# Layer 0's first product takes x unnormalized: the mean moved into the weights, the deviation's factor behind the product

## The chip, the core and the metric

The kernel runs on one core of one Trainium2 chip. The core has five engines with instruction queues of their own: TensorE (PE in the profile; its weight loads are PEld), VectorE (DVE), ScalarE (ACT), GpSimd (POOL) and SyncE (SP), which here only issues DMA transfers. The metric is the time of one execution on the device in microseconds.

## The reference, cut to what matters

Two layers of a graph network with a mixture of experts, on 3327 nodes with 256 features. The layer norm has no weights:

```python
def _layernorm(x, axis=-1, eps=1e-5):
    m = jnp.mean(x, axis=axis, keepdims=True)
    v = jnp.var(x, axis=axis, keepdims=True)
    return (x - m) / jnp.sqrt(v + eps)

def _L0_gnn_ref(x, adj, W, b):
    support = jnp.matmul(x, W)                 # 3327 x 256, the "node features" s
    out = jnp.matmul(adj, support) + b
    return jax.nn.relu(out)

x = x + _L0_gnn_ref(_layernorm(x), adj, W, b)
x = x + _L0_ffn_ref(_layernorm(x), ...)        # 8 experts, top 2, hidden 1024
x = x + _L1_gnn_ref(_layernorm(x), adj, ...)   # tanh filter, top 700, two weights
x = x + _L1_ffn_ref(_layernorm(x), ...)        # 8 experts, top 2, hidden 256
```

What the change touches is the product `matmul(_layernorm(x), W)` of layer 0. For one row, (x - m) r W = r (x W - m 1W), with r = 1/sqrt(v + eps). Since m is the mean of x's row, x W - m 1W = x (W - M), where each column of M holds the mean of that column of W.

## The kernel before

The nodes are padded to 26 tiles of 128 rows. `x` lies in SBUF whole, as 128 partitions x 26 tiles x 256 features in f32, and so does `s`, the node features. The kernel is written in a framework that takes instructions in program order, gives each engine its own queue with a scheduler's order, and puts semaphores between engines. So an engine takes its instructions strictly in its queue's order; an instruction that waits holds up what stands behind it.

The order of the work:

1. SP loads x in seven transfers (L129), four tiles each, the last two; GpSimd loads the weights `proj_sb` (L226, through L213). Then SP fills the ring of six pieces (`ring`, 1664 KB each) with the transposed adjacency (L322).
2. GpSimd makes constants (L132 to L193): an identity for transposes, ones, masks, and counts that VectorE turns into f32 (the casts `blocks` L167, `ids` L184, `spare` L189, `slot` L193). The casts and GpSimd's next step wait for each other, and GpSimd issues small loads (L213 to L223) in between.
3. Layer 0's node features, a loop over pairs of tiles (L952 to L955). For each pair: VectorE takes mean and variance (`bn_stats` L254, `bn_aggr` L255), and one over the deviation by a bit trick and three Newton rounds in twelve more small operations (L257 to L266, tiles `ln_ve`, `ln_half`, `ln_guess`, `ln_nw`); VectorE then writes the normalized tile `xn` (L276); TensorE transposes it in 128x128 blocks to PSUM (L288, `pt`); ScalarE copies it to SBUF (L289, `xnT`); TensorE multiplies by the weights (L296, `ps_s`, two products of 128x256 for a tile), and ScalarE copies the result into `s` (L299). There are two `pt` and two `xnT` buffers, and four PSUM buffers for products (tag `py`).
4. The aggregation over 13 panels of 256 nodes (`aggregate`, L326 to L349): 52 f32 products for a panel from the ring and `s` (L340, `ps_g`), while VectorE normalizes finished tiles and routes them to experts, GpSimd scatters the rows to DRAM, and ScalarE counts positive entries of the adjacency (L962).
5. The experts of layer 0 in blocks of 256 rows (L785, L797, L839), the layer between (`between`, L1090), layer 1's aggregation and its experts.

`node_features` (L292) is called by layer 0's loop and, with other weights, by layer 1 (`second_features`, L1073); `statistics` (L246) is called by all four layer norms. An f32 product of 128x256 stands in the profile as two records.

Of the kernel before, what the change touches and what calls it, by code (L numbers as in the profile page):

```python
# [10 lines left out]
F32 = mybir.dt.float32  # L11
BF16 = mybir.dt.bfloat16
I32 = mybir.dt.int32
AF = mybir.ActivationFunctionType
ALU = mybir.AluOpType
# [7 lines left out]
P = 128  # L23
NT = 26
NP = NT * P
D = 256
DC = D // P
# [6 lines left out]
RING = 6  # L34
# [41 lines left out]


BEGUN, FIRST_TILES = 6, 14
FREE_PAN = NPAN - RING // NCHUNK
assert K * EARLY_PAN * PW >= E * (SB - 1) + EARLY * SB  # L80
PAIRS = [(t, 2) for t in range(0, NT, 2)]
# [4 lines left out]
def gnn_moe_two_layers(  # L86
# [24 lines left out]
    nc = tc.nc  # L111

    const = ctx.enter_context(tc.tile_pool(name="const", bufs=1))
    state = ctx.enter_context(tc.tile_pool(name="state", bufs=1))
    work = ctx.enter_context(tc.tile_pool(name="work", bufs=3))
    dram = ctx.enter_context(tc.tile_pool(name="dram", bufs=1, space=bass.MemoryType.DRAM))
    psh = ctx.enter_context(tc.tile_pool(name="psh", bufs=2, space=PSUM))
    psy = ctx.enter_context(tc.tile_pool(name="psy", bufs=4, space=PSUM))
    pst = ctx.enter_context(tc.tile_pool(name="pst", bufs=2, space=PSUM))

    x = state.tile([P, NT, D], F32, name="x")
    s = state.tile([P, NT, D], F32, name="s")

    ring = [state.tile([P, PIECE], F32, name=f"ring{i}") for i in range(RING)]
    cum = state.tile([P, NT + 1, E], BF16, name="cum")

    for t in range(0, NT, 4):
        n = min(4, NT - t)
        nc.sync.dma_start(out=x[:, t : t + n, :], in_=x_in[:, t : t + n, :])  # L129


    ident = const.tile([P, P], F32, name="ident")  # L132
    make_identity(nc, ident)
    ones = const.tile([P, 1], F32, name="ones")
    nc.gpsimd.memset(ones, 1.0)
    ones_sq = const.tile([P, P], BF16, name="ones_sq")
    nc.gpsimd.memset(ones_sq, 1.0)

    before = const.tile([P, P], BF16, name="before")
    nc.gpsimd.memset(before, 1.0)  # L140
# [1 line left out]
        out=before,  # L142
        in_=before,
# [66 lines left out]
    def by_feature(name, w, t=None):  # L210
        if t is None:
            t = const.tile([P, DC, w.shape[1]], F32, name=name)
        nc.gpsimd.dma_start(out=t, in_=w.rearrange("(c p) n -> p c n", p=P))  # L213
        return t

    def on_all_partitions(name, b):
        t = const.tile([P, b.shape[1]], F32, name=name)
        nc.gpsimd.dma_start(out=t, in_=b.partition_broadcast(P))
        return t
# [3 lines left out]
        nc.gpsimd.dma_start(out=t, in_=a)  # L223
        return t

    proj_sb = by_feature("proj_sb", g0_w)  # L226
    gnn_b_sb = on_all_partitions("gnn_b_sb", g0_b[0:1, :])
    f0_bg_sb = on_all_partitions("f0_bg_sb", f0_bg[0:1, :])
    gate = state.tile([P, E, D], F32, name="gate")
# [16 lines left out]
    def statistics(t0, n, kept=None):  # L246


        st = work.tile([P, n, 6], F32, name="ln_st")
        mv, guess = kept or (  # L250
            work.tile([P, n, 2], F32, name="ln_mv"), work.tile([P, n], I32, name="ln_guess")
        )
        for g in range(n):
            nc.vector.bn_stats(out=st[:, g, :], in_=x[:, t0 + g, :])  # L254
            nc.vector.bn_aggr(out=mv[:, g, :], in_=st[:, g, :])  # L255
        ve = work.tile([P, n], F32, name="ln_ve")
        nc.vector.tensor_scalar(ve, mv[:, :, 1], EPS, None, ALU.add)  # L257
        half = work.tile([P, n], I32, name="ln_half")
        nc.vector.tensor_scalar(half, ve.bitcast(I32), 1, None, ALU.logical_shift_right)
        nc.vector.tensor_scalar(guess, half, -1.0, float(0x5F3759DF), ALU.mult, ALU.add)  # L260
        rs = guess.bitcast(F32)
        nw = work.tile([P, n], F32, name="ln_nw")
        for _ in range(3):
            nc.vector.scalar_tensor_tensor(nw, rs, -0.5, rs, ALU.mult, ALU.mult)
            nc.vector.tensor_tensor(nw, nw, ve, ALU.mult)
            nc.vector.scalar_tensor_tensor(rs, nw, 1.5, rs, ALU.add, ALU.mult)  # L266
        return mv, rs

    def layernorm(t0, n, stats=None, at=0, xn=None):


        mv, rs = stats or statistics(t0, n)
        if xn is None:
            xn = work.tile([P, n, K, RW], F32, name="xn")
        for g in range(n):
            last_normalized[:] = [nc.vector.tensor_scalar(  # L276
                xn[:, g, 0, 0:D], x[:, t0 + g, :], mv[:, at + g, 0:1], rs[:, at + g : at + g + 1],
                ALU.subtract, ALU.mult,
            )]
        return xn  # L280

    def by_features(xn, n):

        xnT = work.tile([P, DC, n * P], F32, name="xnT", bufs=2)
        pt = pst.tile([P, DC, n * P], F32, name="pt", tag="pt")
        for g in range(n):
            for c in range(DC):
                nc.tensor.transpose(pt[:, c, ts(g, P)], xn[:, g, 0, ts(c, P)], ident)  # L288
        nc.scalar.copy(xnT, pt)  # L289
        return xnT  # L290

    def node_features(i, lhsT, w_sb):  # L292

        ps = psy.tile([P, D], F32, name="ps_s", tag="py")
        for c in range(DC):
            nc.tensor.matmul(  # L296
                ps, lhsT=lhsT[:, c, :], rhs=w_sb[:, c, :], start=(c == 0), stop=(c == DC - 1)
            )
        return nc.scalar.copy(s[:, i, :], ps)  # L299

    def add_relu(x_tile, ps, b_sb):

# [273 lines left out]
    def plan_early():  # L576


        early_rows[:] = rows_written
        nb = parts_of(tokens(EARLY_PAN * PW // P), SB - 1, "pl_nb")  # L580
        nb2, base2 = in_tiers(nb, None)
        end, past = steps(nb2, EARLY)
        v = work.tile([P, 3, 2 * E], F32, name="pl_v", bufs=1)
        ids_and_leads(v, nb2, base2, SB)
        sums = sums_before(past, v, EARLY, 2)
        row = work.tile([P, EARLY], F32, name="pl_row", bufs=1)
        nc.vector.tensor_tensor(row, slots[:, 0:EARLY], sums[:, 1, :], ALU.subtract)
        nc.vector.tensor_copy(early_table[:, 0, :], sums[:, 0, :])
        nc.vector.scalar_tensor_tensor(
            early_table[:, 1, :], sums[:, 0, :], float(NP), row, ALU.mult, ALU.add  # L590
        )
        took2 = work.tile([P, 2 * E], F32, name="pl_took2", bufs=1)
        taken(took2, nb2, end, EARLY)
        nc.vector.tensor_tensor(done, took2[:, 0:E], took2[:, E:], ALU.add)
# [105 lines left out]
    def experts(xlist, ys, group, fixed, n_hidden, func, w1T, b1, w2T, b2, copy, kept=None):  # L700
# [23 lines left out]
        def col_of(t):  # L724
            return t if t < EARLY else order[t - EARLY]

        def groups_of(t):
            return SG if t < EARLY or order[t - EARLY] < LATE_PAIRS else 1
# [6 lines left out]
        def load_one(late):  # L735
            t = len(loaded)
            table = late[0] if t >= EARLY else early_table
            col, n = col_of(t), groups_of(t)
            base = FREE_PAN * NCHUNK + t * places

# [196 lines left out]
    def fill(xlist):  # L937

        with tc.issue_after(last_piece[0].ins):
            for e in range(E):  # L940
                zeros = blk.tile([P, H // P, SB], F32, name="wide").rearrange("p h b -> p (h b)")
                zeros = zeros[:, 0 : SG * RW].rearrange("p (g d) -> p g d", g=SG)
                nc.gpsimd.memset(zeros, 0.0)
                nc.gpsimd.tensor_scalar(
                    zeros[:, :, ID], slot, float(AWAY + SPARE + (LATE + e) * SB), None, ALU.add
                )
                nc.sync.dma_start(
                    out=xlist[e * NP : e * NP + SB, :].rearrange("(g p) d -> p g d", p=P),
                    in_=zeros,
                )  # L950

    for t, n in PAIRS:  # L952
        xnT = by_features(layernorm(t, n), n)
        for g in range(n):
            last_feature = node_features(t + g, xnT[:, :, ts(g, P)], proj_sb)  # L955

    def count(pan, chunks):
        with tc.issue_after(last_feature.ins):
# [13 lines left out]
    def after0(pan):  # L972
# [9 lines left out]
        if pan == 1:  # L982
            fill(xlist1)
        if FREE_PAN <= pan < NPAN - 1:
            layer0.load(None)
# [12 lines left out]
    with tc.issue_after(last_product[0].ins):  # L998
# [9 lines left out]
        pc, lhsT=ones, rhs=positive.rearrange("p n i k -> p (n i k)"), start=True, stop=True  # L1008
# [35 lines left out]
    def begin():  # L1044
        for b in begun:
            add_loaded(*b)
        return statistics(0, BEGUN, begun_stats)
# [25 lines left out]
    def second_features(t, xnT):  # L1073
        n = 2
        h2T = work.tile([P, DC, n * P], F32, name="h2T", bufs=2)
        for oc in range(DC):
            ps = psh.tile([P, n * P], F32, name="ps_p", tag="ph")
            for c in range(DC):
                nc.tensor.matmul(  # L1079
                    ps,  # L1080
                    lhsT=proj_sb[:, c, ts(oc, P)],
                    rhs=xnT[:, c, :],
                    start=(c == 0),
                    stop=(c == DC - 1),
                )
            nc.scalar.activation(h2T[:, oc, :], ps, AF.Tanh, bias=g1_bp_sb[:, oc : oc + 1])
        for g in range(n):
            node_features(t + g, h2T[:, :, ts(g, P)], g1_wg_sb)
# [42 lines left out]
    def after1(layer1, pan):  # L1131
# [8 lines left out]
        if pan == EARLY_PAN:  # L1140
            plan_early()
        if FREE_PAN <= pan < NPAN - 1:
            for _ in range(NCHUNK):
# [35 lines left out]
    with tc.If(first_usual > 0) as arms:  # L1179
# [19 lines left out]
        with tc.If(second_usual > 0) as inner:  # L1199
# [6 lines left out]
            while len(layer1.started) < layer1.always:  # L1206
# [6 lines left out]
                if 0 <= k - 3 < len(first_tiles):  # L1213
                    t, n = first_tiles[k - 3]
# [175 lines left out]
```

## Time and profile before

| | |
|---|---|
| runs | 1262.30, 1259.44, 1262.47 us; median 1262.3 |
| profiled execution | 1255.26 us, of which the span from first to last instruction is 1253.5 |
| TensorE busy | 1201.3 us, 96% of the span |
| mean granted TensorE clock | 0.989 |
| layer 0's aggregation starts | 46.57 us into the span |

The span is cut into groups, waits and a chain. The chain of work that ended last is followed back from the last instruction, at each step to what released it. "Busy" of TensorE counts a matmul's record from start to end; records overlap. The granted clock is the share of full speed that the throttle allowed TensorE.

### The profile page before, as it was taken

What the parts mean: (1) busy time and instruction counts of PE and PEld (TensorE: products, weight loads), DVE (VectorE), ACT (ScalarE), POOL (GpSimd) and SP (SyncE); (2) the same over time, 40 slices, a digit from 0 to 9 for tenths busy, and PEclk for the clock granted to TensorE, in tenths of its full rate; (3) what the DMA queues carried; (4) which work ended last, traced back from release to release, by engine and by line L of the source; (5) the groups of instructions that cost most, each with busy time, mean ns of one, the idle gap of its engine ahead of it and who ended that gap; (6) DMA issues with size and microseconds to landing.
All of it is one profiled execution on the core that took longest, in us unless ns stands there. A gap on an engine that the chain in (4) does not pass through costs nothing.

```text
span 1253.5 us, 18523 instructions
## 1 busy us (share of the span) xinstructions
PE 1201.3 (96%) x5816; PEld 1035.3 (83%) x5816; DVE 712.2 (57%) x2919; ACT 519.3 (41%) x963; POOL 289.7 (23%) x363
## 2 busy tenths in 40 slices
PE   6999999999999999999999998999999999999992
PEld 5888888888888888888888887788888888877771
DVE  8267767677663111111111148668999998784454
ACT  3797455541022222323232234995455552043330
POOL 2023122131231111111111110302323223264432
PEclk9999999999999999999999998999999999999996
DMA  9676554454267655757566557244445542477696
GB/s 365 170 248 215 181 181 165 160 198 139 63 228 238 207 178 177 257 173 247 186 224 210 181 203 266 94 164 166 168 171 198 179 147 82 130 243 220 204 272 213
DMA packets 119546, 241.60 MB, mean 193 GB/s; under 512 B 21568, under 2 KB 89936, under 8 KB 112400
## 3 DMA queue, kind: packets, MB, share of 16 engines
q1 hardware_dynamic: 106624, 206.91, 50.3%
q0 software_dynamic: 11184, 31.85, 6.9%
q10 hardware_dynamic: 1632, 1.57, 0.4%
q8 instruction: 48, 0.79, 0.3%
q14 instruction: 58, 0.48, 0.1%
HBM read 203.99 MB, written 36.33 MB: 192 GB/s over the span
## 4 chain that ended last, share of the span: by engine, by line
PE 90%; DMA 4%; DVE 2%; issue 2%; ACT 1%; POOL 0%; SPq 0%; DVEq 0%; ACTq 0%; POOLq 0%
PE ps_g L340 47%; PE ps_y L839 18%; PE ps_h L797 18%; PE ps_s L296 4%; DMA ys<-wide,index 2%; DMA ring<-ys 2%; PE ptb L785 2%; PE ps_p L1079 1%; PE pt L288 1%; DVE x L916 0%; ACT xnT L289 0%; DMA x<-in_x 0%; DVE wide L846 0%; DVE ln_st L254 0%; POOL ys L464 0%
## 5 line engine op out<-in xcount | busy, mean ns | idle before, releaser
L340 PE MATMUL ps_g<-s,ring 128*128 128x256 f32 x2704 | 588.3, 380 | 0.0
L340 PEld LDWEIGHTS ps_g<-s,ring 128*128 128x128 f32 x2704 | 512.0, 190 | 68.7
L797 PE MATMUL ps_h<-xT,ring 128*128 128x256 f32 (+1 forms) x1176 | 252.6, 368 | 1.9 <-DVE xT L788 1.1
L797 PEld LDWEIGHTS ps_h<-xT,ring 128*128 128x128 f32 x1176 | 206.4, 190 | 39.7 <-ACT wide L804 4.7
L804 ACT ACTIVATE wide<-ps_h,ring 128x256 f32<-128x256 f32 (+1 forms) x240 | 110.1, 459 | 286.3 <-PE ps_h L797 278.1
L360 DVE SCALAR_TENSOR_TENSOR rt_product<-xn,gate 128x256 f32<-128x256 f32 x400 | 197.7, 494 | 12.4
L839 PE MATMUL ps_y<-ring,wide 128*128 128x256 f32 x896 | 200.3, 379 | 0.0
L464 POOL DMA_INDIRECT xlist<-xn,rt_idx x104 | 106.6, 1025 | 377.2 <-DVE ln_ve L257 301.7
L839 PEld LDWEIGHTS ps_y<-ring,wide 128*128 128x128 f32 x896 | 167.1, 190 | 21.0
L962 ACT ACTIVATE sign<-ring,below 128x416 bf16<-128x416 f32 x208 | 133.5, 642 | 72.6 <-DMA ring<-in_adjT 66.5
L464 POOL DMA_INDIRECT ys<-narrow,index x56 | 54.5, 972 | 331.4 <-DVE narrow L847 239.3
L788 DVE COPY xT<-ptb 128x512 f32<-128x512 f32 (+1 forms) x29 | 19.2, 663 | 153.5 <-PE ptb L785 153.5
L1110 ACT ACTIVATE ring<-ring 128x3328 f32<-128x3328 f32 x22 | 65.5, 2982 | 90.2 <-PE ps_g L340 37.2
L846 DVE TENSOR_TENSOR narrow<-ps_y,ring 128x256 f32<-128x256 f32 x56 | 23.8, 424 | 134.2 <-PE ps_y L839 132.7
L304 DVE TENSOR_TENSOR gnn_t<-ps_g,gnn_b_sb 128x256 f32<-128x256 f32 x52 | 21.9, 422 | 109.0 <-PE ps_g L340 96.3
L464 POOL DMA_INDIRECT ys<-wide,index x58 | 55.9, 965 | 63.4 <-DVE wide L847 40.3
L1111 ACT ACTIVATE ring<-ring 128x3328 f32<-128x3328 f32 x22 | 65.5, 2982 | 0.6
L804 ACT ACTIVATE narrow<-ps_h,ring 128x256 f32<-128x256 f32 (+1 forms) x64 | 28.9, 453 | 73.2 <-PE ps_h L797 54.7
L839 PE MATMUL ps_y<-s,narrow 128*128 x200 | 49.9, 390 | 5.5 <-issue 3.2
L425 ACT ACTIVATE rt_d<-rt_d 128x2 f32<-128x2 f32 x26 | 5.3, 202 | 115.2 <-DVE rt_d L424 115.2
L916 DVE TENSOR_TENSOR x<-x,ring 128x512 f32<-128x512 f32 (+1 forms) x36 | 30.2, 839 | 32.4 <-DMA ring<-ys 32.0
L839 PEld LDWEIGHTS ps_y<-s,narrow 128*128 128x128 f32 x200 | 35.4, 189 | 14.6 <-issue 8.6
(195 smaller groups left out, 1021.0 us busy)
## 6 DMA issues: line engine op xcount, KB each, us to landing
ring<-in_adjT SPq DMA_DIRECT2D x52, 1664.0 KB, 7.0
ring<-in_f_w1T SPq DMA_DIRECT2D x30, 1024.0 KB, 5.9
ring<-in_f_w2T SPq DMA_DIRECT2D x30, 1024.0 KB, 8.1
ring<-xlist SPq DMA_DIRECT2D x52, 258.0 KB, 2.9
ring<-in_f_w SPq DMA_DIRECT2D x36, 256.0 KB, 3.5
ring<-ys SPq DMA_DIRECT2D x13, 512.0 KB, 5.0
ring<-ys SPq DMA_DIRECT2D x5, 1024.0 KB, 5.5
ring<-in_f_b SPq DMA_DIRECT2D x34, 128.0 KB, 7.2
```

Of the source, the lines that this page charges most:

```text
L296: nc.tensor.matmul(ps, lhsT=lhsT[:, c, :], rhs=w_sb[:, c, :], start=(c == 0), stop=(c == DC - 1))
L340: nc.tensor.matmul(ps[it], lhsT=chunks[k][:, c, ts(it, P)], rhs=s[:, j, :], start=(j == 0), stop=(j == NT - 1),)
L360: nc.vector.scalar_tensor_tensor(product, xn[:, g, 0, 0:D], 1.0, gate[:, e, :], ALU.mult, ALU.mult, accum_out=sc[:, g, e : e + 1],)
L464: d = nc.gpsimd.indirect_dma_start(out=a[:, :], out_offset=bass.IndirectOffsetOnAxis(ap=index, axis=0), in_=rows_, in_offset=None,)
L785: nc.tensor.transpose(pt[:, c, ts(g, P)], xb[:, g, ts(c, P)], ident)
L797: nc.tensor.matmul(ps, lhsT=w1[:, c, ts(hc, P)], rhs=xT[:, c, :], start=(c == 0), stop=(c == DC - 1),)
L804: nc.scalar.activation(hT[:, hc, :], ps, func, bias=bb1[:, hc : hc + 1])
L839: last_product[:] = [nc.tensor.matmul(ps, lhsT=hT[:, hc, ts(g, P)], rhs=w2[:, hc, :], start=(hc == 0), stop=(hc == hc_n - 1),)]
L916: nc.vector.tensor_tensor(x_t, x_t, yt[:, :, k * D : (k + 1) * D], ALU.add)
L962: nc.scalar.activation(sign, a[:, :, ts(i, GROUP)], AF.Sign, bias=below, accum_out=positive[:, pan, i, k : k + 1],)
L1110: nc.scalar.activation(a, a, AF.Square)
L1111: nc.scalar.activation(a, a, AF.Tanh)
```

## The change

There are five parts. The first two tiles of x are loaded by a transfer of their own, then the weights on the same queue, then the rest of x. TensorE multiplies a tile of ones with itself 32 times at the very start, into a PSUM tile that nobody reads. The column means of the weights are made on TensorE (a matrix whose entries are all 1/256, kept for that time in the last piece of the ring, times the weights), and VectorE subtracts them from the weights in place. Layer 0 then transposes x itself, multiplies, and the copy from PSUM to `s` on ScalarE is an activation that multiplies each row by its r. Statistics are taken for batches of 2, 4, 4, 8 and 8 tiles instead of 2. And two temporaries of `statistics` are smaller: `ln_st` holds one tile, `ln_half` shares the space of `ln_nw`. The activation in `node_features` is used by layer 1 too, with a factor of 1.

```diff
+WARM = 32
...
-    for t in range(0, NT, 4):
-        n = min(4, NT - t)
+    proj_sb = const.tile([P, DC, D], F32, name="proj_sb")
+    for t, n in [(0, 2)] + [(t, 4) for t in range(2, NT, 4)]:
         nc.sync.dma_start(out=x[:, t : t + n, :], in_=x_in[:, t : t + n, :])
+        if t == 0:
+            nc.sync.dma_start(out=proj_sb, in_=g0_w.rearrange("(c p) n -> p c n", p=P))
+    ones_sq = const.tile([P, P], BF16, name="ones_sq")
+    nc.gpsimd.memset(ones_sq, 1.0)
+    warm = psy.tile([P, P], F32, name="ps_warm", tag="py")
+    for _ in range(WARM):
+        nc.tensor.matmul(warm, lhsT=ones_sq, rhs=ones_sq, start=True, stop=True)
     ident = const.tile([P, P], F32, name="ident")
     make_identity(nc, ident)
+    mean = ring[RING - 1][:, 0:P]
+    nc.gpsimd.memset(mean, 1.0 / D)
     ones = const.tile([P, 1], F32, name="ones")
     nc.gpsimd.memset(ones, 1.0)
-    ones_sq = const.tile([P, P], BF16, name="ones_sq")
-    nc.gpsimd.memset(ones_sq, 1.0)
...
-    proj_sb = by_feature("proj_sb", g0_w)
...
     def statistics(t0, n, kept=None):
-        st = work.tile([P, n, 6], F32, name="ln_st")
...
         for g in range(n):
-            nc.vector.bn_stats(out=st[:, g, :], in_=x[:, t0 + g, :])
-            nc.vector.bn_aggr(out=mv[:, g, :], in_=st[:, g, :])
+            st = work.tile([P, 6], F32, name="ln_st")
+            nc.vector.bn_stats(out=st, in_=x[:, t0 + g, :])
+            nc.vector.bn_aggr(out=mv[:, g, :], in_=st)
...
-        half = work.tile([P, n], I32, name="ln_half")
+        nw = work.tile([P, n], F32, name="ln_nw")
+        half = nw.bitcast(I32)
...
-        nw = work.tile([P, n], F32, name="ln_nw")
...
     def by_features(xn, n):
+        return turned_tiles([xn[:, g, 0, :] for g in range(n)])
+
+    def turned_tiles(tiles):
+        n = len(tiles)
         xnT = work.tile([P, DC, n * P], F32, name="xnT", bufs=2)
         pt = pst.tile([P, DC, n * P], F32, name="pt", tag="pt")
         for g in range(n):
             for c in range(DC):
-                nc.tensor.transpose(pt[:, c, ts(g, P)], xn[:, g, 0, ts(c, P)], ident)
+                nc.tensor.transpose(pt[:, c, ts(g, P)], tiles[g][:, ts(c, P)], ident)
         nc.scalar.copy(xnT, pt)
         return xnT

-    def node_features(i, lhsT, w_sb):
+    def node_features(i, lhsT, w_sb, scale=1.0):
...
-        return nc.scalar.copy(s[:, i, :], ps)
+        return nc.scalar.activation(s[:, i, :], ps, AF.Copy, scale=scale)
...
-    for t, n in PAIRS:
-        xnT = by_features(layernorm(t, n), n)
-        for g in range(n):
-            last_feature = node_features(t + g, xnT[:, :, ts(g, P)], proj_sb)
+    deviation = {}
+    for t0, n0 in [(0, 2), (2, 4), (6, 4), (10, 8), (18, 8)]:
+        _, rs = statistics(t0, n0)
+        deviation.update((t0 + g, rs[:, g : g + 1]) for g in range(n0))
+        for t in range(t0, t0 + n0, 2):
+            xT = turned_tiles([x[:, t + g, :] for g in range(2)])
+            if t == 0:
+                ps = psy.tile([P, D], F32, name="ps_mean", tag="py")
+                for c in range(DC):
+                    nc.tensor.matmul(
+                        ps, lhsT=mean, rhs=proj_sb[:, c, :], start=(c == 0), stop=(c == DC - 1)
+                    )
+                nc.vector.tensor_tensor(
+                    proj_sb, proj_sb, ps.unsqueeze(1).to_broadcast([P, DC, D]), ALU.subtract
+                )
+            for g in range(2):
+                last_feature = node_features(
+                    t + g, xT[:, :, ts(g, P)], proj_sb, deviation[t + g]
+                )
```

## The prediction

> **What bounds the kernel now.** I read the page first. TensorE is busy 96% of the span, and the chain that ended last is 90% TensorE. So a change that touches only the first 46 us can bring no more than what it takes from TensorE's idle or slow time there.
>
> ```profile
> span 1253.5 us, 18523 instructions
> PE 1201.3 (96%) x5816; PEld 1035.3 (83%) x5816; DVE 712.2 (57%) x2919; ACT 519.3 (41%) x963; POOL 289.7 (23%) x363
> PE 90%; DMA 4%; DVE 2%; issue 2%; ACT 1%; POOL 0%; SPq 0%; DVEq 0%; ACTq 0%; POOLq 0%
> ```
>
> Second, the chain in order of time over the first 110 us (start, length, what):
>
> ```profile
> 0.81 3.97 DMA x<-in_x
> ...
> 9.30 0.65 DVE xn L276 x2
> ...
> 11.42 0.42 DVE xn L276
> ...
> 11.89 1.11 PE pt L288 x4
> 13.00 5.97 PE ps_s L296 x16
> 18.96 0.45 PE pt L288 x4
> ...
> 19.50 0.59 ACT xnT L289
> 20.09 0.04 issue
> 20.14 3.72 PE ps_s L296 x16
> ...
> 46.57 44.89 PE ps_g L340 x208
> ```
>
> Three things are to be seen. x lands at 4.78, but the first product starts at 13.0, after VectorE's statistics and a detour to GpSimd. The products of tiles 0 to 3 (eight products, two records each) take 5.97 us where the next four tiles take 3.72: TensorE is at half pace until about 17.9. From 20.14 on each round of four tiles costs 4.89 us, and from 46.57 the aggregation runs without a gap. So the prize is how much earlier than 20.14 the products of tiles 4 to 7 start; everything behind shifts by that.
>
> Third, what idleness does to TensorE later: the windows from 756.4, where it waits for statistics between the layers (granted clock third from the end).
>
> ```profile
> 756.40:757.40 1.00, 0.01 (x1) 0.00 (x0) 1.00 (x6) 0.37 (x1) 0.00 (x0) 1.00 1.01 426
> 757.40:758.60 1.20, 0.00 (x0) 0.00 (x0) 1.06 (x7) 0.00 (x0) 0.00 (x0) 1.00 1.12 477
> 758.60:759.60 1.00, 0.00 (x0) 0.00 (x0) 0.83 (x6) 0.00 (x0) 0.00 (x0) 0.52 0.78 311
> 762.60:765.40 2.80, 2.80 (x9) 2.22 (x8) 2.73 (x8) 1.06 (x2) 0.00 (x0) 0.50 1.05 447
> ```
>
> Work ended at 756.4; by 758.6, 2.2 us later, the clock was halved; work resumed at 760.9 and the full clock came back at 765.4, 4.5 us after.
>
> **The change, part by part.** *Loads.* Two tiles of x go first, then the weights, on SP's queue. Before, 512 KB landed at 4.78, 0.9 us after that many bytes had moved (windows of the first 5 us: 66, 106, 246, 352, 385 GB/s in half-microseconds from 1.5). 256 KB had moved at 3.15, so two tiles land at about 4.1 and the weights at 4.8; the next tiles follow at 413 GB/s (6.1, 7.3, 8.6), ahead of need. The sixth ring load now waits for the mean products; only two small gate loads stand right behind it, ring data is not read before 40 us, and the transfers were saturated to 38 us anyway: nothing. On SP one more issue pushes the later loads back by its own 0.4 to 0.7 us, ahead of need; GpSimd loses an issue of 0.92 at 2.73, which nothing waits behind, and gains one 0.2 us memset: nothing.
>
> *Warming products.* 32 bf16 128x128 products from 1.05 (ones_sq is now GpSimd's first memset; memsets ended by 1.2 before). The trace has no such product. Lower bound 0.05 us each (bf16 products of 8 columns start 0.025 apart at full clock), upper 0.27 (first four f32 transposes, 1.09 us). I take 0.12: f32 transposes stand 0.45/4 = 0.11 apart at full clock, bf16 half of that, half clock twice. 32 x 0.12 = 3.8, so TensorE is free at 4.9; by the bounds at 2.7 or 9.7.
>
> *Mean products.* Two f32 products (four records at 0.43 slow, plus 0.2 drain): 1.9 us, 4.9 to 6.8. VectorE's queue reaches the subtraction at 4.1 + 0.80 (two bn_stats at 0.33 and an aggregate) + 7 dependent small operations at 0.20 = 6.3. So the subtraction starts at s = 6.8 and takes 0.65 (PSUM copies of that size 0.66). Transposes run 6.8 to 7.9, the copy on ScalarE ends near then, and the products of tiles 0 to 3 run from 8.0, at full clock (TensorE has been occupied since 1.05), to 11.7; transposes of 4 to 7 until 12.7. Until there the gain is 18.96 - 11.7 = 7.3 us.
>
> *The deviation behind the product: a new wait.* ScalarE's copies of s now carry the factor, and in the built order its queue reads: s of tiles 0, 1, then 2, 3, which wait for VectorE, and only then xnT of tiles 4 to 7. Statistics of tiles 2 to 5 are one batch, and its last operation is number 61 in VectorE's queue. Behind s: subtraction 0.65, six bn_stats at 0.33, fourteen small ones at 0.07 give 3.5 to the cast "blocks". Then the casts ids, spare and slot each wait for GpSimd, which in between issues DMAs:
>
> ```profile
> 10.13 0.26 POOL L172 TENSOR_SCALAR starts<-blocks 128x8 f32<-128x8 f32 x1 [6.48 <-DVE ln_nw L265]
> 10.89 0.25 POOL L182 IOTA wide_i<- 128x52 int32 x1
> 11.96 0.58 POOL L218 DMA_DIRECT2D f_bg_sb<-in_f_bg  x1
> 12.53 0.73 POOL L213 DMA_DIRECT2D f_r_sb<-in_f_rT  x1
> 13.26 0.16 POOL L191 IOTA wide_i<- 128x2 int32 x1
> ```
>
> Before, blocks to slot took 9.95 to 13.45 = 3.5 us; the new order (f_bg and f_r now ahead of the second iota) keeps the sum. The batch's rest is 1.2. Together s + 8.3. Then two s copies at 0.36 and one xnT copy of 0.59, with gaps 1.4: tiles 4 to 7 start at s + 9.7 = 16.5, against 20.14: 3.6 us earlier. Later batches (10.5 and 14.2 behind s) come before their tiles.
>
> *The clock.* TensorE then waits from 12.7 to 16.5, 3.8 us. By the row above, the clock is halved 2.2 us into such a gap and returns 4.5 us after work resumes. Of a 4.89 us round 3.72 are products, so the loss is 4.5 x 1/2 x 0.76 = 1.7. Bounds: 0 and 2.25 (5.97 - 3.72). I take 1.8, since tiles 4 to 7 meet the clock as the first four did.
> [...]
>
> *xn's scaling gone, ScalarE's copies.* 26 normalizations (0.33 each) leave VectorE; it was no longer the limit after 20 us, so nothing. COPY 128x256 takes 375 ns, ACTIVATE of that shape 473: 0.10 more for each s copy. In layer 0 ScalarE idles 0.49 before each, hidden. In layer 1 the same helper runs 26 times: 0 to 2.6 us; ScalarE is full only in 789 to 805 (9.82 of 10 us in 790 to 800), six copies there, half on the chain: 0.3.
>
> *Statistics' temporaries* (ln_half shares ln_nw, ln_st per tile) add no wait on another engine: nothing. The built order of the rest is unchanged but for one xlist load on SP.
>
> **Sum.** 3.6 - 1.8 - 0.3 = 1.5 us. The profiled execution took 1255.26 (1253.5 span and 1.8 around it); the runs' median is 1262.3, 0.6% above, so I take the difference off the median: 1260.8.
>
> **Rivals.** *Clock kept*: the gap is too short, or the first four tiles run slow themselves and fill it. For: warming products may not count as work, then tiles 0 to 3 end near 14 and the gap shrinks to about 1.5 us, while the start at 16.5 stays. Against: the 756 row. Gain 3.6 - 0.3 = 3.3, up to 4.3 if the mean products run fast too and x lands a little earlier: 1258 to 1259.
>
> *No wait for the statistics*: VectorE's batch comes in time, tiles 4 to 7 start 1.18 behind the first four (as 18.96 to 20.14 now), at 12.9: 7.2 - 0.3 = 6.9 us, 1255.4. For: the casts need not stall if GpSimd's issues are quicker. Against: without any stall the batch still ends at s + 7.3, so most of the wait stays.
>
> *Warming holds TensorE* (slower): at 0.27 each TensorE is free at 9.7, s is 11.6, tiles 4 to 7 start at 21.3, 1.2 later than now, with the slow clock 1.8 and 0.3: 3.3 slower, 1265.6, and 1267.9 with all layer-1 copies on the chain. It decides from 0.17 a product, where the gain is gone. For: TensorE starts slow. Against: bf16, and 0.025 between small ones.
>
> That the change does nothing is out: the built order has no xn in layer 0, and the first product's waits are changed as it says.
>
> **How the numbers follow.** The sum's case 0.40, clock kept 0.26, no wait 0.21, warming holds 0.13. What a measurement of this kernel can tell from no change is about 0.3%, 3.8 us: "no wait" and the upper half of "clock kept" (0.13) lie beyond it, and I count the slower case as beyond it too. Faster 0.34, same 0.53, slower 0.13. The range runs from 1255.2 to 1265.0; outside lie half of "no wait" and half of the slower case.
>
> **What would show it.** In the profile after: the first ps_s at about 8, not 13; 16 records in 3.7 us; then a TensorE wait of 3 to 4 us ended by ScalarE's xnT, itself behind s copies that wait for VectorE's ln_guess; clock 0.5 around 16 to 21; ps_g starting at 44 to 45. Wrong if ps_g starts below 41 (no wait), or above 46 (warming holds), or if a gap opens after 46 that is not there now.

## The result, and the profile after

The changed kernel takes 1262.39 us (median of 12 runs, 1260.0 to 1263.7), the kernel before in the same comparison 1262.38 (12 runs, 1259.44 to 1263.58). The ratio is 0.9997 with a 95% interval of 0.9989 to 1.0005: no difference that can be measured. The prediction said 1260.8, held no measurable change for the likeliest outcome, and its range held the time. But its sum of 1.5 us gained lies just outside the interval (which allows 1.4 gained at most), and the trace says more exactly that the sum failed: the aggregation starts half a microsecond later than before, not 1.8 earlier.

The page first: the same bound as before.

```profile
span 1260.6 us, 18469 instructions
PE 1207.1 (96%) x5852; PEld 1040.0 (82%) x5852; DVE 699.9 (56%) x2798; ACT 521.9 (41%) x963; POOL 289.5 (23%) x363
PE 90%; DMA 3%; issue 2%; DVE 2%; ACT 1%; POOL 1%; SPq 0%; POOLq 0%; ACTq 0%; DVEq 0%
```

The chain in order of time over the first 48 us of the changed kernel (start, length, what):

```profile
1.73 5.69 DMA x<-in_x
7.45 0.43 DVE ln_st L262
...
14.00 1.55 DVE slot L202
...
16.42 0.13 DVE ln_guess L274 x2
16.56 0.07 ACT s L311
...
16.93 0.47 ACT s L311
17.40 0.49 ACT xnT L301
17.93 6.45 PE ps_s L308 x16
...
25.54 3.73 PE ps_s L308 x16
...
47.08 1.08 PE ps_g L352 x5
```

This is the chain that the prediction described: statistics of tiles 2 to 5 in VectorE's queue, then the copies of `s`, then `xnT`, then TensorE. Tiles 4 to 7 start at 17.93 (20.14 before), but at half pace: 6.45 us for a round that takes 3.73 from 25.54 on. TensorE's timeline of the same stretch (start, duration, operation, in brackets the idle time before and its releaser) shows both the early success and the gap:

```profile
7.96 3.62 PE L308 MATMUL ps_s<-proj_sb,xnT 128*128 128x256 f32 x16
11.42 1.04 PE L300 MATMUL pt<-ident,x 128*128 128x128 f32 x8
17.93 6.44 PE L308 MATMUL ps_s<-proj_sb,xnT 128*128 128x256 f32 x16 [5.47 <-ACT xnT L301]
```

Tiles 0 to 3 run at 7.96 in 3.62 us (12.79 and 6.17 before, by the same view), so 7.5 us are won by 12.46, where the last transposes end. The gap of 5.47 us and the slow round behind it take all of it back.

The profiled spans differ by 7 us (1260.6 against 1253.5), but hardly from the change: layer 1's aggregation starts at 805.73 against 805.39. The stretch from there to the end is 454.9 against 448.1. It goes with the set of runs and not with the kernel: in the changed kernel's set both kernels take 1262 us, and in the later runs the stretch is 447 to 450 in eight profiles of two sets, 457 to 459 in the three of the third, whose runs of the kernel before also took 1265 us where those of the other sets took 1255. So experiments are judged here by the start of the two aggregations in their traces, and by ratios to runs of the kernel before on the same chip.

### The profile page after: what moved, and what is told of

The parts are those of the page before. It is cut to its first block, busy times and chain, and to the rows that moved or that the text cites. A ratio compares the mean times of both kernels' runs of the same rounds, so it can differ in the third digit from the quotient of the medians.

```text
span 1260.6 us, 18469 instructions
## 1 busy us (share of the span) xinstructions
PE 1207.1 (96%) x5852; PEld 1040.0 (82%) x5852; DVE 699.9 (56%) x2798; ACT 521.9 (41%) x963; POOL 289.5 (23%) x363
## 3 DMA queue, kind: packets, MB, share of 16 engines
q10 hardware_dynamic: 1632, 1.57, 0.4%
## 4 chain that ended last, share of the span: by engine, by line
PE 90%; DMA 3%; issue 2%; DVE 2%; ACT 1%; POOL 1%; SPq 0%; POOLq 0%; ACTq 0%; DVEq 0%
PE ps_g L352 46%; PE ps_y L851 18%; PE ps_h L809 18%; PE ps_s L308 3%; DMA ring<-ys 2%; PE ptb L797 2%; PE ps_p L1109 1%; DMA ys<-wide,index 1%; POOL ys L476 1%; DMA x<-in_x 0%; PE pt L300 0%; ACT xnT L301 0%; DVE x L928 0%; ACT s L311 0%; DVE ln_st L262 0%
## 5 line engine op out<-in xcount | busy, mean ns | idle before, releaser
L437 ACT ACTIVATE rt_d<-rt_d 128x2 f32<-128x2 f32 x26 | 5.3, 202 | 119.7 <-DVE rt_d L436 119.7
```

## The experiments

The table collects what the runs below showed: start and length of the products of tiles 4 to 7, the first `ps_g` of layer 0, the `ps_g` that opens layer 1's unbroken aggregation (all from TensorE's timeline, us), and, where timed, the ratio to the kernel before.

| kernel | tiles 4-7 | layer 0's `ps_g` | layer 1's | ratio (95%) |
|---|---|---|---|---|
| before | 20.14, 3.72 | 46.41 | 805.23 | |
| changed | 17.93, 6.44 | 46.91 | 805.56 | 0.9997 (0.9989 to 1.0005) |
| no factor | 13.80, 3.72 | 40.07 | 804.68 | 0.9987 (0.9975 to 1.0) |
| no warming | 18.90, 5.50 | 46.95 | 805.28 | |
| products in the gap | 18.43, 3.72 | 44.70 | 802.94 | 0.9992 (0.9983 to 1.0001) |
| casts moved + small batches | 14.70, 3.72 | 42.03 | 802.00 | 0.9984 (0.9964 to 1.0003) |
| casts moved | 17.68, 6.60 | 46.83 | 806.81 | |
| small batches | 16.77, 5.41 | 44.72 | 804.43 | |
| clearing doubled | 19.42, 6.14 | 48.12 | 806.54 | |
| no factor + SP's loads moved | 13.28, 3.72 | 39.55 | 798.21 | 0.995 (0.9935 to 0.9964) |
| SP's loads moved | 18.66, 5.88 | 47.09 | 806.93 | |
| both edits, finer, SP's loads moved | 14.51, 3.72 | 41.84 | 800.26 | 0.9961 (0.9948 to 0.9975) |
| the same, statistics paced | 13.12, 3.72 | 39.86 | 799.42 | 0.9945 (0.993 to 0.996) |

**Without the factor.** Is the gap the new wait for the deviation's factor, and what is the early start worth without it?

```diff
-                    t + g, xT[:, :, ts(g, P)], proj_sb, deviation[t + g]
+                    t + g, xT[:, :, ts(g, P)], proj_sb
```

> The deviation's factor is left out of the copies of s in layer 0 (the statistics are still computed, nothing waits for them), so layer 0's features are not scaled. In the changed kernel TensorE stood still from 12.46 to 17.93 and then ran tiles 4 to 7 in 6.45 us. Theory (the new wait for the factor takes the gain): no gap over 1 us, tiles 4 to 7 start at 12.9 and take 3.7, ps_g starts at 39.5 to 40 instead of 47.08, and the time falls by about 7 us, to 1255 to 1256. Rival (the early start meets another bound, x's later tiles or the ring's data): a new gap of 3 us or more opens between 13 and 46, ps_g starts at 43 or later. Rival (the gain is given back behind the first stage): ps_g at 40, but the time is within 2 us of the kernel before.

The gap is gone, and the first aggregation starts 6.8 us earlier than in the changed kernel. That part of the theory held. The time fell by only 0.13% (1.6 us, interval 0 to 3.1), not by 7: the second rival is right in what it says of the time, with a cause that no theory had named. It shows in TensorE's timeline ahead of the fifth panel, whose products start at 134.88:

```profile
107.70 22.69 PE L352 MATMUL ps_g<-s,ring 128*128 128x256 f32 x104
134.66 0.18 PE L458 MATMUL pr<-rt_both,before 128*128 128x8 bf16 x1 [4.27 <-DVE rt_both L409]
...
134.88 24.38 PE L352 MATMUL ps_g<-s,ring 128*128 128x256 f32 x104
```

The wait costs 4.27 us, and the panel behind it 1.69 more (24.38 for 22.69). Of the 6.8 us that leaves 0.9, which is what is left at layer 1 (804.68 against 805.56).

SP's queue (start, duration, transfers) shows where the wait comes from:

```profile
15.97 25.35 SPq L1008 DMA_DIRECT2D gate<-in_f_rT  x1
41.43 26.56 SPq L959 DMA_DIRECT2D xlist<-wide  x5
68.09 0.69 SPq L334 DMA_DIRECT2D ring<-in_adjT  x1
...
93.66 9.53 SPq L959 DMA_DIRECT2D xlist<-wide  x4
103.29 4.87 SPq L334 DMA_DIRECT2D ring<-in_adjT  x3
```

The issue of a gate load of 8 KB stands in the queue from 15.97 to 41.32, and 16 zero lists (GpSimd clears a buffer, SP writes it to DRAM), interleaved with ring loads, follow. In the lists of waits SP stands 35.3 us for GpSimd's `wide` (L956, up to 110 us), and GpSimd 42.3 us for earlier lists to land (L955, 12 times from 60 to 165), since there are two `wide` buffers. So a ring load is issued at 103.29 and lands at 111.67. ScalarE counts that piece from 111.75 on, and the small operation `rt_d` (L437, at 117.76) stands behind it in its queue. VectorE's routing waits for `rt_d` (18.1 us), and TensorE for VectorE.

**Without the warming products.** What do the 32 constant products buy?

```diff
-WARM = 32
+WARM = 0
...
-    warm = psy.tile([P, P], F32, name="ps_warm", tag="py")
     for _ in range(WARM):
-        nc.tensor.matmul(warm, lhsT=ones_sq, rhs=ones_sq, start=True, stop=True)
+        pass
```

> The 32 constant products at the start are left out; nothing else differs from the changed kernel. Theory (tiles 4 to 7 are held by the statistics, not by TensorE): the mean products start when x and the weights have landed, at about 4.5, so the subtraction stays within 0.3 of 6.56; tiles 0 to 3 take about 6 us instead of 3.62 and end at 14; tiles 4 to 7 start at 17.9 all the same, ps_g at 46.5 to 47.3. Rival (the warming is what brings the early start): everything from the first product on comes 2.3 or more later, ps_g at 49 or later.

The start of the aggregation is as expected (46.95 against 46.91), but by two misses that cancel. TensorE's timeline:

```profile
4.65 2.04 PE L975 MATMUL ps_mean<-proj_sb,ring 128*128 128x256 f32 x4 [4.65 <-DMA proj_sb<-in_g_w]
6.48 1.06 PE L299 MATMUL pt<-ident,x 128*128 128x128 f32 x4
7.87 1.11 PE L299 MATMUL pt<-ident,x 128*128 128x128 f32 x4 [0.33 <-DMA x<-in_x]
8.78 3.67 PE L307 MATMUL ps_s<-proj_sb,xnT 128*128 128x256 f32 x16
```

Tiles 0 to 3 are at full pace at 8.78 without any warming; I expected about 6 us for them. TensorE did nothing before 4.65; the mean products went at half pace (2.04 us), and 4.1 us after its first work it is at full pace, with nothing but the mean products and the transposes of x ahead. In three other runs, with the 32 products, the mean products took 1.10 us instead of 2.04, but then TensorE waited 2 us and more for x. The cost of the 32 is as small as their use, since without them TensorE waits for the weights till 4.65 anyway. Tiles 4 to 7 start at 18.90, 1.0 later than expected (VectorE waited 1.38 us for the fourth load of x, tiles 10 to 13), and lose less of the clock (5.50 against 6.44).

**Products in the gap.** Does the gap cost the clock?

```diff
+            if t == 2:
+                again = psh.tile([P, D], F32, name="ps_fill", tag="ph")
+                for _ in range(AGAIN):            # 4
+                    for c in range(DC):
+                        nc.tensor.matmul(
+                            again, lhsT=xT[:, c, P:], rhs=proj_sb[:, c, :],
+                            start=(c == 0), stop=(c == DC - 1),
+                        )
```

> Behind the products of tile 3 these products are done four times more, into a tile of PSUM that nobody reads: 16 records, 3.7 us at full clock, inside the gap of 5.47 us. Theory (the gap costs 2.7 us of clock on top of itself): the idle stretches left are 1.6 us or shorter, the granted clock stays at 1.0, tiles 4 to 7 start at 17.9 as before and take 3.7 instead of 6.45, ps_g starts at 44.3, the time falls by 2.7 us. Rival (the clock's fall does not come from the gap): tiles 4 to 7 take 6.4 again, ps_g stays at 47.

```profile
15.45 1.04 PE L301 MATMUL pt<-ident,x 128*128 128x128 f32 x8
18.43 3.72 PE L309 MATMUL ps_s<-proj_sb,xnT 128*128 128x256 f32 x16 [1.95 <-ACT xnT L302]
```

The round takes 3.72 instead of 6.44, though it starts 0.5 later (x landed later in this execution), and the aggregation starts at 44.70 (44.3 expected). In the trace the gain is still there at layer 1 (802.94, 2.6 less than in the changed kernel). The timed gain, 0.08% (1.0 us of the 2.7 expected), is too small for its interval to exclude zero. Work that nobody needs thus brings 2.2 us (44.70 against 46.91), only by keeping TensorE busy.

**Casts moved and small batches, together and apart.** What in VectorE's queue makes the factor late?

```diff
-    nc.vector.tensor_copy(blocks, count_i)        # and ids, spare, slot
+    nc.gpsimd.tensor_copy(blocks, count_i)
...
-    for t0, n0 in [(0, 2), (2, 4), (6, 4), (10, 8), (18, 8)]:
+    for t0, n0 in [(0, 2), (2, 2), (4, 2), (6, 4), (10, 8), (18, 8)]:
```

> The statistics of tiles 2 and 3 and of tiles 4 and 5 are two batches instead of one, and the four casts blocks, ids, spare and slot run on GpSimd instead of VectorE, so that no wait for GpSimd stands in VectorE's queue ahead of the factors. Theory (the queue ahead of the factors is what holds TensorE): the factor of tiles 2 and 3 is there at 12 to 12.7 instead of 16.5, tiles 4 to 7 start at 13 to 14 at full clock; a second, shorter gap of up to 2 us may open ahead of tiles 8 to 11, whose copies stand behind the factors of tiles 6 to 9; ps_g at 39.7 to 42, the time 5 to 7 us less than before. Rival (VectorE is slow in 13 to 16 whatever its queue holds, or GpSimd with the casts becomes late): tiles 4 to 7 start at 16 or later, ps_g at 45 or later.

Both together: tiles 4 to 7 start at 14.70 at full pace, the next round after a second gap of 1.35 (up to 2 was expected), `ps_g` at 42.03. The first and the last lie 0.7 and 0.03 beyond the theory's upper ends, far from the rival's 16 and 45. Of the 4.9 us won there, 3.6 are left in layer 1 (802.00), since the wait ahead of the fifth panel appears here too (1.36 us at 133.71). The timed gain, 0.16% (2.0 us), misses the 5 to 7 us expected, and its interval does not exclude zero.

The casts alone:

> Only the four casts blocks, ids, spare and slot go from VectorE to GpSimd; the statistics' batches are those of the changed kernel (factor of tiles 2 and 3 at 16.54 there). Theory (the casts and their waits hold the batch): VectorE saves two waits of 1.07 together, four casts of 0.5 or, with the slowed one, 2.1: the factor is there at 13.4 to 15, tiles 4 to 7 start at 14.8 to 16.4, ps_g at 42 to 46. Rival (the smaller batches did it all in the run with both edits): tiles 4 to 7 start at 17 or later.

Tiles 4 to 7 start at 17.68, the rival's number. Without the casts VectorE meets another hold at once, 1.52 us for the fourth load of x (tiles 10 to 13), whose statistics stand in its queue ahead of the last operations of the batch of tiles 2 to 5. That load landed at 13.66 in this execution; in the changed kernel's profile its statistics began at 11.90 without a wait. Without the 1.52 us the start would be 16.2 (an estimate by subtraction), inside the theory's range: this single execution does not decide between the two. This run also had the wait ahead of the fifth panel (1.12 us at 138.28), though its aggregation started no earlier: its ring load that stood at 99.04 in the changed kernel was issued at 106.88.

The batches alone:

> Only the batches of the statistics are smaller (2, 2, 2, 4, 8, 8 tiles); the casts stay on VectorE. Theory (two holds in one queue: the casts with GpSimd, and the batch with its late x; each alone suffices, as the run with the casts moved alone showed, where tiles 4 to 7 started at 17.68): the factor of tiles 2 and 3 still stands behind the cast slot and the slowed operations, is there at 15.6 to 16.2, tiles 4 to 7 start at 16.9 to 17.7, ps_g at 45.5 to 47. Rival (the batch alone is the hold): tiles 4 to 7 start at 14.7 as in the run with both, ps_g at 42 to 43.

Tiles 4 to 7 start at 16.77 and `ps_g` at 44.72, 0.1 and 0.8 below the theory's lower ends; the start is far from the rival's 14.7. So neither edit alone did it in these executions, and together they brought more than the sum of both (tiles 4 to 7 are 3.2 earlier; apart 0.3 and 1.2). That fits holds that stand one behind the other in one queue. The sizes are rough: each is one execution, and the fourth load of x landed at least 1.8 us later in one than in another.

**Clearing doubled.** In the changed kernel three operations behind the cast `slot`, and the cast itself, end only at 15.55. VectorE's timeline:

```profile
13.92 1.63 DVE L202 CAST slot<-wide_i 128x2 f32<-128x2 int32 x1
13.97 1.57 DVE L274 SCALAR_TENSOR_TENSOR ln_guess<-ln_nw,ln_guess 128x4 f32<-128x4 f32 x1
14.05 1.51 DVE L269 TENSOR_SCALAR ln_guess<-ln_nw 128x4 int32<-128x4 int32 x1
14.12 1.44 DVE L263 BATCH_NORM_AGGREGATE ln_mv<-ln_st 128x2 f32<-128x6 f32 x1
```

GpSimd's timeline at the same time:

```profile
13.69 0.76 POOL L222 DMA_DIRECT2D g_wg_sb<-in_g_wg  x1
...
14.51 1.01 POOL L955 MEMSET wide<- 128x516 f32 x2
```

```diff
                 nc.gpsimd.memset(zeros, 0.0)
+                nc.gpsimd.memset(zeros, 0.0)
```

> Each clearing of a zero list on GpSimd (128x516, 0.55 us) is done twice; nothing else differs from the changed kernel. There three operations of VectorE on 2 to 8 bytes per partition took 1.4 to 1.6 us each while GpSimd cleared the first two lists at 14.51 to 15.52, the first of them from 13.92, while GpSimd issued a load. Theory (VectorE's small operations wait for GpSimd's clearing): the clearings now run from 14.5 to 16.5, those operations end about 1.0 later, at 16.5, and tiles 4 to 7 start at about 18.9, ps_g at 48. Rival (the load's issue, not the clearing, holds VectorE): they end at 15.5 as before, tiles 4 to 7 start at 17.9, ps_g at 47.1.

```profile
14.49 2.56 DVE L202 CAST slot<-wide_i 128x2 f32<-128x2 int32 x1
14.55 2.50 DVE L274 SCALAR_TENSOR_TENSOR ln_guess<-ln_nw,ln_guess 128x4 f32<-128x4 f32 x1
```

The cast takes 0.93 us more, with two more clearings of 1.01 together on GpSimd (four from 15.08 to 17.02), and ends 0.03 after the last. So the clearing does hold it. Tiles 4 to 7 start at 19.42, 1.5 later than in the changed kernel; 0.6 of that was there before (the cast starts at 14.49 instead of 13.92, after a later landing of x). What the run does not separate is the load's issue ahead of the clearing: the cast starts during it in both runs.

Other traces answer that in part, and show that the hold is not only the cast's. First VectorE and GpSimd in the run with small batches, then both in the last version below, whose casts are on GpSimd:

```profile
15.31 1.07 DVE L268 TENSOR_SCALAR ln_nw<-ln_ve 128x4 int32<-128x4 int32 x1
15.35 1.01 POOL L955 MEMSET wide<- 128x516 f32 x2
8.38 0.86 DVE L267 TENSOR_SCALAR ln_ve<-ln_mv 128x2 f32<-128x2 f32 x1
8.69 0.53 POOL L957 MEMSET wide<- 128x516 f32 x1
```

Both are `tensor_scalar` operations without a cast ahead, and both end 0.02 after a clearing. With small batches the cast `slot` itself took only 0.47 and ended at 14.57 together with a load's issue on GpSimd, before any clearing; so an issue can hold it too, though the cast `spare` ran in 0.19 us during another issue (13.24). A `scalar_tensor_tensor` was not held: in the run with both edits two of them took 0.14 us each during the clearings (8.12 to 9.21).

**SP's loads moved.** Is SP's queue what gave the gain back in the run without the factor?

```diff
-                for name, w in (("gate0", f0_wgT), ("gate1", f1_rT)):
-                    ...
+                gate_rows("gate0", f0_wgT)        # the same load
...
-        if pan == 1:
+        if pan == 3:
+            with tc.issue_after(last_piece[0].ins):
+                gate_rows("gate1", f1_rT)
+        if pan == 5:
             fill(xlist1)
```

> As the run without the factor (layer 0's copies of s unscaled), and on SP's queue the second gate load is moved from behind panel 0 to behind panel 3, and the zeros for layer 1's list from panel 1 to panel 5. In the run without the factor, ps_g started at 40.07, 7.0 earlier than in the changed kernel, but its third panel at 134.88, only 2.3 earlier, after a wait of 4.27, and the fourth at 159.20, 0.6 earlier: a ring load stood behind the gate load (SP's queue 15.97 to 41.32) and four zero lists and was issued at 103.29. Theory (SP's queue is the next bound): that load is issued before 80, no wait over 0.5 us in 60 to 160, the third panel starts at 130.3, the fourth at 152.9, the second layer's ps_g at 798 to 799, and the time is 6 to 7 us under the kernel before. Rival (VectorE's or ScalarE's own work on a panel is the next bound): a wait of 2 us or more is still there ahead of the third or fourth panel, and the time is within 3 us of the kernel before.

```profile
107.18 22.69 PE L352 MATMUL ps_g<-s,ring 128*128 128x256 f32 x104
129.82 22.69 PE L352 MATMUL ps_g<-s,ring 128*128 128x256 f32 x104
152.45 12.76 PE L352 MATMUL ps_g<-s,ring 128*128 128x256 f32 x58
```

The wait is gone and layer 1 starts at 798.21, 7.0 under the kernel before; the time is 0.50% less (6.3 us, 4.5 to 8.2). This is SP's queue, shown: the ring load that was issued at 103.29 is issued at 84.67 (before 80 was expected). Which of the two moved loads matters more was not tried apart, but SP's queue shows that the hold up to 41 us is not the gate load's own:

```profile
16.43 25.14 SPq L959 DMA_DIRECT2D xlist<-wide  x1
```

With the gate load gone, the first zero list waits in its place, until 41.57. In the changed kernel, where the gate load stands till 41.14, the transfers move 413 to 434 GB/s from 20 to 38 us and 14 GB/s from 40 to 42 us. (The expectation counted panels from the first long stretch: its third is the fifth of 13.) The same move on the changed kernel, factor kept:

> The changed kernel with the second gate load and layer 1's zeros moved on SP's queue, and nothing else. Theory (that queue binds only where the aggregation starts early, or where the queue itself runs late, as with the casts moved alone: ps_g at 46.83 and a wait of 1.4 before 138): ps_g starts at 46.5 to 47.5, the second layer's at 805 to 806, no gain over 0.5 us. Rival (the moved loads cost or bring time by themselves): the stretch from the first ps_g to the second layer's, 758.65 in the changed kernel, changes by over 1 us.

`ps_g` starts at 47.09, as expected; layer 1's at 806.93, 0.9 beyond the range. The stretch between is 759.84, 1.2 more than in the changed kernel, which would speak for the rival; but the run with small batches in the same set, without moved loads, has 759.71. So most of the 1.2 goes with the set, and the moved loads alone show no gain or cost above 0.2 us.

**The version that the runs point to.** Both edits, finer batches and moved loads:

> The factor is kept. Casts on GpSimd, statistics in batches of 2, 2, 2, 2, 2, 4, 4 and 8 tiles, and the second gate load and layer 1's zeros moved on SP's queue to panels 3 and 5. The run with both first edits had waits of 1.54 ahead of tiles 4 to 7 and 1.35 ahead of tiles 8 to 11, ps_g at 42.03, and a wait of 1.36 ahead of the third panel. Theory: the second of those waits goes (smaller batch), the third goes (SP's queue), ps_g at 40.5 to 41.5, no wait over 0.5 us in 60 to 160, the second layer's ps_g at 799 to 801 (805.39 in the kernel before), the time 4 to 6 us under the kernel before. Rival (the smaller batches' extra operations make VectorE late for the tiles behind, or the moved loads hold the ring later): a wait of over 1 us ahead of tiles 8 to 25, or one of over 1 us between 160 and 300; the time within 3 us of the kernel before.

0.39% less than before (4.9 us, 3.1 to 6.5). `ps_g` starts at 41.84, 0.3 later than expected: the finer batches did not close the second gap (1.36 again), as VectorE's queue still takes later tiles' statistics first. So the last version holds them back:

```diff
+    factors = []
-    for t0, n0 in [(0, 2), (2, 2), (4, 2), (6, 2), (8, 2), (10, 4), (14, 4), (18, 8)]:
-        _, rs = statistics(t0, n0)
+    for t0, n0 in [(0, 2), (2, 2), (4, 2), (6, 2), (8, 2), (10, 4), (14, 4), (18, 4), (22, 4)]:
+        with tc.issue_after(factors[-2].ins) if len(factors) > 1 else nullcontext():
+            _, rs = statistics(t0, n0)
+        factors.append(last_rs[0])                # the batch's last operation
...
```

> As the version with both edits and the moved loads, but a batch's statistics are issued only behind the last operation of the batch before the last one, so that later tiles' statistics no longer stand ahead of the factors that TensorE waits for; batches of 2, 2, 2, 2, 2, 4, 4, 4, 4. There the waits ahead of tiles 4 to 7 and 8 to 11 were 1.54 and 1.36, ps_g at 41.84. Theory (what is left is the order in VectorE's queue): the factor of tiles 2 and 3 is there at 12 instead of 13.1, tiles 4 to 7 start at 13.3 to 13.8, tiles 8 to 11 with a wait under 0.8; ps_g at 39.6 to 41, the second layer's at 798.3 to 799.7, the time 5 to 7 us under the kernel before. Rival (the batches' dependent operations, now less overlapped, are too slow for a round of 4.89): waits of over 1 us appear ahead of tiles 12 to 25, ps_g at 42 or later.

```profile
13.12 3.72 PE L310 MATMUL ps_s<-proj_sb,xnT 128*128 128x256 f32 x16 [0.81 <-ACT xnT L303]
18.01 3.72 PE L310 MATMUL ps_s<-proj_sb,xnT 128*128 128x256 f32 x16 [0.29 <-ACT xnT L303]
23.37 3.72 PE L310 MATMUL ps_s<-proj_sb,xnT 128*128 128x256 f32 x16 [0.77 <-ACT xnT L303]
...
39.86 10.31 PE L354 MATMUL ps_g<-s,ring 128*128 128x256 f32 x47
```

No gap over 0.81 is left, the clock stays, and the time is 0.55% less than before (7.0 us, 5.1 to 8.9): faster than the kernel before and than the changed one, whose intervals against the same kernel do not meet. Layer 1 starts at 799.42, 5.8 under the kernel before's profile.

## Why the prediction was right or wrong, point by point

*What bounds the kernel, and the gap.* Right: the new wait, its place in ScalarE's queue and its releaser are as written, and without the factor the gap is gone. "Same" came out for the reason given, an early start that is given back; all of it, where I had three fifths of the 3.6 us given back. That the range held the time says little: it is 9.8 us wide, and the whole gain of the sum was 1.5.

*Loads.* The weights were there for the mean products at 4.48 (4.8 said). The second load of x landed at 7.42, not 6.1: the step took 413 GB/s for each load in turn. That load decides when statistics of tiles 2 to 5 begin (7.45), and behind the subtraction I had none of that wait. In ten of the eleven other runs VectorE waited 0.3 to 1.4 us for it.

*Warming and mean products.* Sizes right: 0.112 us each (3.59 for 32; 0.12 said, with half of f32's time for bf16 as my estimate: four f32 transposes at half pace, from 11.89 in the kernel before, stand 0.23 apart), 2.04 (1.9 said), the subtraction at 6.56 and 0.69 long (6.8, 0.65), tiles 0 to 3 at 7.96 (8.0). Wrong in its reason: "at full clock (TensorE has been occupied since 1.05)". They are at full pace without the warming too (3.67 us in the run without it). The slower rival was priced on warming that holds TensorE from 0.17 a product on; at 0.112 it was far from deciding.

*The wait's size: the step that failed.* Factors at s + 8.3 were said; with s = 6.56 that is 14.9, and they were there at 16.54, 10.0 behind s. Two of the three terms held: 3.7 us to the start of `blocks` (3.5 said, though its own parts add up to 3.6), and 3.7 from there to the start of `slot` (10.25 to 13.92; 3.5 said). The third, "the batch's rest is 1.2", took 2.6 (13.92 to 16.54), since the cast `slot`, held by GpSimd, took 1.63 us. The row to see it by was in VectorE's timeline of before, 1.40 us for two writes of `xn` that take 0.72 to 0.83 elsewhere:

```profile
13.98 1.40 DVE L276 TENSOR_SCALAR xn<-x,ln_mv,ln_guess 128x256 f32<-128x256 f32 x2
```

GpSimd issued a load and cleared two buffers beside it (13.91 to 15.84). The change removes this operation, but the hold passed to the next operation of VectorE's queue that meets GpSimd. The gap was thus 5.47, not 3.8.

*The clock.* The mechanism is right: the gap of 5.47 lost 2.7 us, and the run with products in it lost none. Against the rival's "too short" for the predicted 3.8 stand the row at 756, halved after 2.2 us, and the gap of 3.67 with small batches, which lost 1.7. The size was 1.8; the bound of 2.25 that I took from the first tiles of before was passed as well. Windows of the changed kernel (granted clock third from the end):

```profile
16.50:17.00 0.50, 0.00 (x0) 0.00 (x0) 0.50 (x4) 0.44 (x2) 0.00 (x0) 0.64 0.75 298
23.00:23.50 0.50, 0.50 (x2) 0.41 (x2) 0.39 (x4) 0.05 (x1) 0.00 (x0) 0.53 0.94 399
```

It was halved at about 16.64 and came back at 23.47: 4.2 us into the gap and 5.5 after work resumed, where the row at 756 had 2.2 and 4.5. So nearly the whole round fell into it.

*ScalarE's copies in layer 1.* 0.3 was said, from 0.10 more for each copy. That price is right in layer 0, where the factor is a column (474 ns against 372); in layer 1, with a factor of 1, a copy takes 384 ns, 0.01 more. The stretch from layer 0's first `ps_g` to layer 1's is 758.65 against 758.82 before: nothing measurable.

*The sum.* 46.57 - 1.8 gave 44.8 for the first `ps_g`; it came at 47.08, 2.3 later. 1.4 is the later start of tiles 4 to 7 (17.93 for 16.5), 0.9 the clock (2.7 for 1.8). My bound, wrong if `ps_g` starts above 46, was crossed, but not through the mechanism that I had tied it to.

*The rivals.* "No wait for the statistics" was priced at 6.9 us by "everything behind shifts by that". The run without the factor starts the first aggregation 6.3 us earlier than the kernel before, and the time falls by 1.6: SP's queue was a second bound close behind, for which the prediction has no term. With SP's loads moved as well, 6.9 earlier became 6.3 in the time. "Clock kept" is the run with products in the gap: 2.3 us at layer 1 against before, the price given was 3.3 to 4.3.

## What to carry to other kernels

When an edit moves a result from ahead of a product to behind it, the wait moves to the engine that drains the product (here ScalarE's copy of `s` waited 6.19 us for VectorE's factor): read that engine's queue, and the queue that feeds it, operation by operation, with every hold that another engine puts on it. An idle stretch of TensorE costs more than itself where the clock falls (here 5.47 us idle, then a round of 6.44 for 3.72), so look for the slow round behind it. And before a shift at the start is counted in full, look one stage on for a transfer queue that has little slack; here 1.6 us without the factor became 6.3 only with the loads moved.

## What the runs showed that I had not expected

*How late the clock falls, and for how long.* The time from the last work to the halving was 2.2 us (at 756), 4.2 (changed kernel) and 4.4 (clearing doubled, at 17.54). With small batches alone, it fell only at 18.04, 1.3 us after work had resumed behind a gap of 3.67, and the round took 5.41. The windows there:

```profile
18.00:18.50 0.50, 0.50 (x3) 0.41 (x2) 0.50 (x6) 0.41 (x1) 0.00 (x0) 0.54 1.03 405
21.00:21.50 0.50, 0.50 (x3) 0.41 (x2) 0.50 (x4) 0.41 (x1) 0.00 (x0) 0.55 0.84 346
```

The halved stretch was 6.83 us long in six profiles (at 756 in the kernel before, the changed kernel, no warming, casts moved, clearing doubled, SP's loads moved) and 3.41, half of that, with small batches (18.04 to 21.45). In the run without the factor the panel behind the gap of 4.27 lost 1.69 us, as the round did with small batches. So the loss does not follow the gap's length: gaps of 3.67 to 6.32 us lost 1.7 to 2.9 us, and the longest was not the dearest. What sets the moment of the fall was not shown. Idle stretches of 2.17 us and less among layer 0's products lost nothing in any run. And the profile's clock reads 1.00 from 13 to 17.9 in the kernel before, where products run at half pace (6.17 us for a round of 3.72), and from 4.5 to 6.5 in the run without warming (2.04 us for mean products of 1.10): there only the durations tell.

*A cast of two columns that takes 1.6 us.* It is held through GpSimd's clearing (1.63 us beside two clearings, 2.56 beside four), and what stands behind it is held with it (1.44 to 1.57 us, and 2.36 to 2.50). Moving the casts away is no full cure: a `tensor_scalar` of two columns was held in the same way (0.86 us in the last version), a `scalar_tensor_tensor` was not (0.14 us beside a clearing in the run with both edits). Why the one is held and the other not was not shown.

*The second issue behind the six ring loads* stands in SP's queue for 24 to 27 us, till 40 to 45 us, whether it is a gate load of 8 KB or a zero list of 258 KB; the same gate load, issued at 107.69, took 0.55 us. What holds it, the ring's transfers or the first gate load ahead of it, was not tried apart.
